# Adding the residual y on VectorE instead of by TensorE transposes, with two new work orders

## The chip, the cores and the metric

The kernel runs on one core of a Trainium2 chip, in float32. The metric is device microseconds of one launch; the median over runs is compared. Engines are named as the profile names them: PE is TensorE (PEld its weight loads), DVE is VectorE, ACT is ScalarE, POOL is GpSimd, and SP issues most of the DMAs.

## The reference, cut to what matters

Two layers follow each other on x of shape (4, 64, 64, 256): four batches of 4096 tokens with 256 channels. The first is a self-attention over the 4096 tokens of a batch with a residual. The second is triangle attention with 8 heads, a residual, a layer norm, an MLP and a second layer norm.

```python
# layer 0, per batch
s = einsum('bqd,bkd->bqk', g, f); beta = softmax(s); o = (beta @ v) @ Wo + bo
y = x + o
# layer 1, per batch
scores = einsum('bilhd,bljhd->biljh', q, k) / sqrt(32); att = softmax(scores, axis=2)
out = einsum('biljh,bilhd,bljhd->bijhd', att, v1, v2)
h = y + out.reshape(B, N, N, E) @ Wo1
h = layer_norm(h) * ln_agg_g + ln_agg_b
z = relu(h @ W1 + b1) @ W2 + b2 + h
result = layer_norm(z) * ln_out_g + ln_out_b
```

The change concerns the line `h = y + ...`: y is held with channels on the partitions, and the heads' product has tokens there, so y has to be turned before it is added.

## The kernel before, in words

The program is one list of instructions for each engine, written in a fixed order (`tc.manual_schedule()`); every engine works through its own list in order and waits on semaphores. For each batch b there is an attention stage (`layer0`) and a triangle stage (`first_layer1` for b = 0, `next_layer1` for b = 1 to 3). A closing stage (`Tokens.alone`) ends the program.

**Attention stage.** 8 blocks of 512 queries (`qb`), each of 8 groups (`k`, counted through as `g`). A group makes scores `s` on PE (L552), exponentials `e` on ACT (L564, buffers of tag `k8`, two of them), products `o` on PE (L579), and a running sum `esum` on DVE (L586). The work that follows a block is spread over the groups of the next block by the list `parts`: normalisation at k = 0 (`norm`, with the sums split in two by L594 to L596 into the one buffer of tag `hid`), `output` at k = 1, where DVE makes y (L632) and SP stores it to DRAM with channels as rows (L635), and projections q, k, v1 and v2 for the triangle stage at k = 2 to 7. In batch 0 DVE also turns the later batches' x by 32x32 blocks (L356). In batches 2 and 3, `recall`, `settle`, `rooted`, `polished`, `scaled` and `finish` bring back the MLP results of the batch two before and do their last layer norm; before the change one 256-token tile goes through them every 3 groups. `finish` is the last scale and shift, two operations on POOL (L1287, L1288) and a store to the output.

**Triangle stage.** 32 steps: 4 pairs of heads times 8 groups of 8 rows. A step has 8 products R = att x v2 of 128x2048 (`product`, L1007, words `R`); for batches 1 to 3 DVE makes 5 and POOL 3 in an even step, and 6 and 2 in an odd one. PE sums each with a 32-column stationary tile (`accumulate`, L1017, words `A`). R has 3 buffers for DVE and 2 for POOL. DVE also makes the softmax sums (`sums`, L932 and L934, words `S`), ACT the weights (`W`), PE turns them (`t`).

**Tokens.** Beside the steps of batch b, the 16 tiles (256 tokens each) of batch b-1 go through the second half of layer 1. `load` fetches a tile's attention output A and, before the change, `yc`, its y with channels on the partitions. `heads` (words h0, h1) makes `hp` in PSUM: two products with Wo1 for each half (L1120), and then two matmuls with the identity (L1125) that turn y and add it in the same accumulation. `sa` makes mean and variance: in batches 1 and 2 by sums on ACT (`sums_of`), in the last stage by bn_stats on DVE. Then `rr`, `pp` (small steps on ACT and POOL), `fa` (normalise), `ht`, `hT` (turn and scale), `m`, `r` (first MLP product, ReLU), `z` (second). In batches 1 and 2 the results are stored (`carried_off`, `summed_off`) and finished in a later attention stage; in the last stage they are finished at once, with `finish` on POOL.

**Order.** In the triangle stages the lists ORDER and ORDER_LAST say in which order the words of one period (two steps and one tile) are written; `/1` or `/2` means that the word works on the period one or two before, `/-1` on the one after. 20 periods are written. First and second tile of a batch have their heads in the last part of `layer0`.

**Closing stage.** `alone` takes the last batch's tiles 2 to 15 through heads, MLP and both norms, one per iteration, with the tiles' `A` and y fetched far ahead.

Of the kernel before, what the change touches and what calls it, by code (L numbers as in the profile page):

```python
# [18 lines left out]
P = 128  # L19
# [24 lines left out]
    R03/2 R06/2 t1/2 h0 m0/1 R04/2 c1/2 A03/2 A07/2 R16/2 A04/2 A06/2 R12/2 R10/2 T00/2 fi/2 W0/1 sf/2 R17/2  # L44
    T01/2 A10/2 A12/2 t0/1 R11/2 r0/1 fo/2 R13/2 R15/2 f1/2 h1 m1/1 f0/2 A11/2 c0/1 A16/2 V0/1 R14/2 r1/1 A13/2
    A15/2 R00/1 A17/2 T10/2 A14/2 sp/1 R02/1 sa R05/1 e0/1 R01/1 z0/1 rr/1 T11/2 z1/1 pp/1 e1/1 so/1 A00/1 A05/1
    R07/1 W1/1 A02/1 A01/1 fa S1 ht V1/1 S0 hU hT
# [4 lines left out]
    r0/1 A10/2 A11/2 m1/1 R14/2 R05/1 S1/1 R15/2 T10/2 sp/1 A14/2 A16/2 r1/1 e0/1 e1/1 A15/2 A05/1 T11/2 R04/1  # L52
    A04/1 z0/1 W1/1 R03/1 V1/1 fi/2 S0 z1/1 t1/1 so/1 R06/1 R00/1 c1/1 sa A03/1 R07/1 R02/1 A06/1 A02/1 A00/1
    rr/1 pp/1 W0 R01/1 A07/1 A01/1 fo/1 fa T01/1 R12/1 t0 T00/1 R17/1 h1/-1 sf/1 R13/1 h0/-1 f0/1 ht f1/1 R16/1
    hU A13/1 hT A12/1 A17/1 R11/1 c0 R10/1 m0 V0
# [19 lines left out]
def attention_then_triangle_kernel(  # L75
# [44 lines left out]
    nc.gpsimd.memset(back_t, -1.0)  # L120
    nc.gpsimd.memset(back_t[:, 2:4], -16.0)
# [85 lines left out]
    dens = ctile([P, NB, 256 + 16], "dens")  # L207
# [238 lines left out]
    class Late:  # L446
# [5 lines left out]
        def load(self, q):  # L452
            self.y = []
            for cc, tag in enumerate(("A", "yc")):
                t = work.tile([P, 512], F32, tag=tag, name="yb", bufs=1)
                nc.sync.dma_start(out=t, in_=self.io["y"][ts(cc, P), ts(q, 512)])
                self.y.append(t)
            self.used = 0
# [39 lines left out]
    def layer0(b, F, safe, rest, ahead):  # L498
# [8 lines left out]
        io["v1"] = dram.tile([T, C], F32, tag="v1", name="v1d")  # L507
        L = Layer1(b, io, safe)
# [105 lines left out]
        def bounds(qb):  # L614
            for j, (t, op) in enumerate(ends.pop(qb)):
                if not safe:
                    c0 = 256 + 2 * qb + j
                    nc.vector.tensor_reduce(dens[:, b, c0 : c0 + 1], t, AX.X, op)
# [7 lines left out]
        def output(qb):  # L626
            col = ts(qb, QB)
            o = oT.pop(qb)
            for cc in range(2):
# [5 lines left out]
                nc.sync.dma_start(out=io["y"][ts(cc, P), col], in_=y(qb, cc))  # L635

# [91 lines left out]
        if late:  # L728
# [4 lines left out]
            parts[7] = [lambda qb: proj(qb, "k", 1)]  # L733
        last = NQB - 1
        for r in range(4):
            score(0, r)
        for g in range(8 * NQB):
# [22 lines left out]
            if b > 1:  # L760
                for do, late in ((rest.finish, 7), (rest.scaled, 6), (rest.polished, 5), (rest.rooted, 4), (rest.settle, 3), (rest.recall, 0)):
                    if (g - late) % 3 == 0 and 0 <= g - late < 3 * NP:
                        do(NP * (b - 2) + (g - late) // 3)
# [29 lines left out]
        bounds(last)  # L793
        proj(last, "v2", 0, None, stage[1][:, 0, :], nc.scalar)
# [55 lines left out]
    class Layer1:  # L850
        def __init__(self, b, io, safe):
# [5 lines left out]
            self.R, self.begun, self.acc, self.rec, self.e = {}, {}, {}, {}, {}  # L857

# [62 lines left out]
        def sums(self, step):  # L921
# [8 lines left out]
            else:  # L930
                den = dens[:, self.b, ts(step, IG)]
# [112 lines left out]
    class Tokens:  # L1044
        def __init__(self):
            self.ios = []
            self.A, self.htp = {}, {}
# [47 lines left out]
        def load(self, tt, far=False):  # L1095
# [4 lines left out]
            if far:  # L1100
# [3 lines left out]
                A, yc = both[:, 0].rearrange("p c (i j) -> p c i j", j=N), both[:, 1]  # L1104
            else:
                A = work.tile([P, 2, 4, N], F32, tag="A", name="A", bufs=1)
                yc = work.tile([P, 2, 256], F32, tag="yc", name="yc", bufs=1)
# [3 lines left out]
            nc.sync.dma_start(out=yc, in_=io["y"][:, ts(t, 256)].rearrange("(c p) t -> p c t", p=P))  # L1111
            self.A[tt] = A, yc

        def heads(self, tt, n, psum=pb, new=None):
# [3 lines left out]
            A, yc = self.A[tt]  # L1118
            for cc in range(2):
                nc.tensor.matmul(  # L1120
                    hp[:, n, :], A[:, cc, ts(n, 2), :].rearrange("p i j -> p (i j)"), wo1_sb[:, cc, :],
                    start=(cc == 0), stop=False,
                )
            for cc in range(2):
                nc.tensor.matmul(  # L1125
                    hp[:, n, ts(cc, P)], yc[:, cc, ts(n, P)], ident, start=False, stop=(cc == 1),
                    is_transpose=True,
                )
# [10 lines left out]
        def stats_a(self, tt):  # L1139
# [539 lines left out]
```

## Time and profile before

| | |
|---|---|
| time, median of 3 runs | 3630.94 us (3627.85 to 3633.84) |
| profiled execution | 3633.17 us, of which the span is 3631.4 us |
| PE busy | 3522.3 us, 97% |
| DVE busy | 2823.5 us, 78% |
| ACT, POOL busy | 1923.8 us, 1779.2 us |
| PE clock granted | 0.994 |

The stages stand at about 0 to 470 us (attention, batch 0), 470 to 860 (triangle 0), 860 to 1300 (attention 1), 1300 to 1730 (triangle 1), 1730 to 2155, 2155 to 2580, 2580 to 3018 (attention 3), 3018 to 3480 (triangle 3, the last) and 3480 to the end (closing stage).

In a timeline line the first number is the start and the second the length in microseconds, and `xN` counts merged instructions. In a line of a group, "busy" counts each moment once, and "mean ns of one" is the length of one instruction, which can overlap its neighbours'. Matmuls in float32 are two PE instructions each; transposes are one.

### The profile page before, as it was taken

How to read it: one execution, taken by the hardware profiler on the slowest of the kernel's cores; microseconds unless marked ns; L12 is line 12 of the kernel's file. 1: busy time of each engine (PE TensorE's matmuls, PEld its weight loads, DVE VectorE, ACT ScalarE, POOL GpSimd, SP SyncE). 2: the span in 40 equal slices, each digit the busy share in tenths (PEclk: the TensorE clock that was granted, in tenths of full speed). 3: DMA queues.
4: the chain of work that ended last, by engine and by line, in shares of the span. 5: the costliest groups of instructions: out<-in, count | busy, mean ns of one | idle time of the engine just before them, and what ended most of it. 6: DMA issues, size and time to landing. Idle time of an engine off the chain costs nothing.

```text
span 3631.4 us, 58644 instructions
## 1 busy us (share of the span) xinstructions
PE 3522.3 (97%) x22282; PEld 1895.3 (52%) x22282; DVE 2823.5 (78%) x2558; ACT 1923.8 (53%) x4221; POOL 1779.2 (49%) x904
## 2 busy tenths in 40 slices
PE   9999999988999999999999999999899999999998
PEld 6555444434555555554455555554455555555477
DVE  4777499996555569999777549999877756999976
ACT  3444455544444366665444446666444436777655
POOL 5000099995000068889211018889611106999920
PEclk9999999999999999999999999999999999999999
DMA  9544555455111354425423254343622235441221
GB/s 174 135 131 127 136 151 137 122 134 136 47 52 52 82 145 108 101 68 107 110 91 95 67 146 109 89 104 76 132 87 95 80 93 134 92 96 46 68 68 55
DMA packets 492594, 370.15 MB, mean 102 GB/s; under 512 B 303184, under 2 KB 434000, under 8 KB 483472
## 3 DMA queue, kind: packets, MB, share of 16 engines
q1 hardware_dynamic: 443264, 339.36, 34.8%
q0 software_dynamic: 36160, 19.94, 5.3%
q10 hardware_dynamic: 12880, 7.01, 0.7%
q8 instruction: 178, 2.92, 0.4%
q14 instruction: 112, 0.92, 0.1%
HBM read 205.73 MB, written 160.43 MB: 101 GB/s over the span
## 4 chain that ended last, share of the span: by engine, by line
PE 67%; POOL 8%; DVE 6%; issue 4%; ACT 1%; DMA 1%; SPq 0%; ACTq 0%; POOLq 0%; DVEq 0%
PE o L579 16%; PE acc L1017 16%; POOL Rp L1007 7%; PE proj L646 6%; PE mp L1253 5%; PE zp L1273 5%; PE s L552 4%; PE sp L905 3%; PE hp L1120 3%; DVE R L1007 2%; PE v1p L678 2%; PE att L959 1%; PE y L631 1%; DVE rec L608 1%; PE htp L1220 1%
## 5 line engine op out<-in xcount | busy, mean ns | idle before, releaser
L1007 POOL TENSOR_TENSOR Rp<-attP,v 128x2048 f32<-128x2048 f32 x328 | 1491.4, 4579 | 409.7 <-ACT attP L967 367.0
L1007 DVE TENSOR_TENSOR R<-att,v 128x2048 f32<-128x2048 f32 x696 | 1546.1, 2279 | 68.6 <-PE acc L1017 49.9
L579 PE MATMUL o<-e,v 128*128 128x512 f32 x2048 | 1043.9, 593 | 0.0
L586 DVE TENSOR_TENSOR esum<-esum,e 128x2048 f32<-128x2048 f32 x224 | 518.8, 2316 | 398.4 <-ACT e L564 395.9
L564 ACT ACTIVATE e<-s 128x1024 f32<-128x1024 f32 x512 | 522.3, 1023 | 529.2 <-PE s L552 438.7
L552 PE MATMUL s<-gT,fT 128*128 128x512 f32 x1024 | 786.7, 770 | 8.7 <-ACT e L564 4.7
L1017 PE MATMUL acc<-R,wsel 128*32 128x512 f32 x5568 | 702.8, 599 | 26.5 <-DVE R L1007 19.6
L579 PEld LDWEIGHTS o<-e,v 128*128 128x128 f32 x2048 | 388.2, 190 | 276.8 <-issue 234.0
L1027 ACT COPY ao<-acc 128x1024 f32<-128x1024 f32 x256 | 256.4, 1013 | 290.4 <-PE acc L1017 205.8
L1017 PE MATMUL acc<-Rp,wsel 128*32 128x512 f32 x2624 | 344.3, 596 | 25.6 <-POOL Rp L1007 23.2
L1017 PEld LDWEIGHTS acc<-R,wsel 128*32 128x32 f32 x5568 | 155.5, 109 | 393.7 <-issue 273.9
L552 PEld LDWEIGHTS s<-gT,fT 128*128 128x128 f32 x1024 | 194.5, 190 | 244.7 <-issue 230.8
L1287 POOL TENSOR_TENSOR hz<-hz,log_bc 128x512 f32<-128x512 f32 x32 | 47.1, 1471 | 542.8 <-ACT hz L1197 474.4
L1181 POOL TENSOR_SCALAR nt<-mv 128x2 f32<-128x2 f32 (+1 forms) x49 | 9.4, 192 | 565.2 <-DVE mv L1137 560.1
L942 ACT ACTIVATE es<-S,rd 128x64 f32<-128x64 f32 x1024 | 258.3, 338 | 15.0 <-DVE rd L934 13.1
L1253 PE MATMUL mp<-hT,w 128*128 128x256 f32 x1024 | 244.4, 384 | 1.7 <-ACT hT L1225 1.7
L1273 PE MATMUL zp<-w,hid 128*128 128x256 f32 x1024 | 239.4, 384 | 0.8 <-ACT hid L1262 0.8
L1253 PEld LDWEIGHTS mp<-hT,w 128*128 128x128 f32 x1024 | 186.5, 190 | 53.0 <-ACT attP L967 12.6
L1273 PEld LDWEIGHTS zp<-w,hid 128*128 128x128 f32 x1024 | 188.0, 190 | 47.8 <-issue 14.7
L608 DVE RECIPROCAL rec<-den 128x512 f32<-128x512 f32 x32 | 107.4, 3357 | 109.7 <-PE den L604 104.4
L1017 PEld LDWEIGHTS acc<-Rp,wsel 128*32 128x32 f32 x2624 | 80.7, 110 | 214.1 <-issue 144.9
L915 ACT ACTIVATE S<-sp 128x512 f32<-128x512 f32 x128 | 131.6, 1094 | 78.0 <-PE sp L905 78.0
(192 smaller groups left out, 3688.4 us busy)
## 6 DMA issues: line engine op xcount, KB each, us to landing
v<-v2d SPq DMA_DIRECT2D x44, 512.0 KB
v1c<-v1d SPq DMA_DIRECT2D x128, 128.0 KB
aT<-ao SPq DMA_DIRECT2D x1024, 16.0 KB
A<-aT SPq DMA_DIRECT2D x256, 64.0 KB
hz<-raw SPq DMA_DIRECT2D x32, 512.0 KB
y<-yT SPq DMA_DIRECT2D x56, 256.0 KB
q<-st SPq DMA_DIRECT2D x56, 256.0 KB
k<-st SPq DMA_DIRECT2D x52, 256.0 KB
```

The source lines that it names most:

```text
L552: nc.tensor.matmul(s_ps[r // 2][:, r % 2, :], fT[tt][:, ts(r * 4 + n, P)], gT[qb // 4][:, ts(qb % 4, QB)], start=True, stop=not safe,)
L564: nc.scalar.activation(e[g][:, 2 * j : 2 * j + 2, :], s_ps[j], AF.Exp)
L579: nc.tensor.matmul(o_ps[qb], F.v[tt][:, r * 4 + n, :], es[:, r, :], start=(k == 0 and r == 0), stop=(k == 7 and r == 3),)
L586: nc.vector.tensor_tensor(esum[qb], esum[qb], es, ALU.add)
L608: nc.vector.reciprocal(rec, den)
L646: nc.tensor.matmul(ps, w[:, cc, rows], y(qb, cc), start=(cc == 0), stop=(cc == 1))
L942: nc.scalar.mul(e[:, i, :], rows[:, i, :], rec[:, i : i + 1])
L1007: eng.tensor_tensor(R, src.unsqueeze(1).to_broadcast([P, D, N]), v2[h], ALU.mult)
L1017: nc.tensor.matmul(acc[32 * c : 32 * c + 32, n % 2, :], w[:, n, c, 16 * h : 16 * h + 32], R[:, ts(c, 8), :].rearrange("p d j -> p (d j)"), ...
L1027: nc.scalar.copy(self.ao[step][:, ts(np, 2)].rearrange("p k d j -> p k (d j)"), self.acc[step][np])
L1253: nc.tensor.matmul(self.mp[:, fc % 2, :], w1_sb[:, cc, ts(fc, P)], self.hT[tt][:, cc, :], start=(cc == 0), stop=(cc == 1),)
L1273: nc.tensor.matmul(zp[:, n, :], self.hid[tt][:, fc, ts(n, P)], w2_sb[:, fc, :], start=(fc == 0), stop=(fc == 3 and tt not in self.hT2),)
```

## The change

- In `layer0`, `turn_y` lets DVE turn each block of y: 8 transposes of 128x128 elements by 32x32 blocks, at k = 5 of the next block, into a tile of tag `hid`. SP then stores it by 4 DMAs to a new DRAM tensor `yt`, with tokens as rows, in pieces of 64 channels (256 bytes). The last block's tile takes a `k8` buffer, and its 4 DMAs are issued by `L.owed()` at the second period of the triangle stage.
- `load` fetches `yt` (tokens on the partitions, two buffers) in place of `yc`. `heads` has no identity matmuls. `add_y` adds y to `hp` in PSUM on DVE, two operations of 128x256 ahead of the mean and variance of each tile, in all triangle stages and the closing stage.
- In the last triangle stage `sa` sums on ACT, as in batches 1 and 2. The last scale and shift of its 16 tiles is no longer done there: the tiles are stored, and `alone` brings back two per iteration and finishes them on POOL.
- In the attention stages of batches 2 and 3, two tiles go through the recalled work in each block at set groups (recall at k = 0 and 1, settle at 3 and 4, finish of both at 7).
- ORDER and ORDER_LAST are new lists; a special case for the first period of the last stage is gone. The softmax sums of a batch are reduced to limits once per batch, instead of all at the end.

```diff
 ORDER = """
-    R03/2 R06/2 t1/2 h0 m0/1 R04/2 c1/2 A03/2 A07/2 R16/2 A04/2 A06/2 R12/2 R10/2 T00/2 fi/2 W0/1 sf/2 R17/2
-    T01/2 A10/2 A12/2 t0/1 R11/2 r0/1 fo/2 R13/2 R15/2 f1/2 h1 m1/1 f0/2 A11/2 c0/1 A16/2 V0/1 R14/2 r1/1 A13/2
-    A15/2 R00/1 A17/2 T10/2 A14/2 sp/1 R02/1 sa R05/1 e0/1 R01/1 z0/1 rr/1 T11/2 z1/1 pp/1 e1/1 so/1 A00/1 A05/1
-    R07/1 W1/1 A02/1 A01/1 fa S1 ht V1/1 S0 hU hT
+    sa R11/2 A13/2 A10/2 A11/2 T01/2 R12/2 sp/1 r0/1 e0/1 e1/1 t0/1 m1/1 R14/2 A12/2 A17/2 fo A14/2 R00/1 V0/1
+    R16/2 T10/2 r1/1 A16/2 c0/1 S1/1 W1/1 rr/1 R07/1 R15/2 A00/1 A15/2 z1/1 R01/1 T11/2 z0/1 pp/1 t1/1 R03/1
+    A01/1 R02/1 so/1 fa A07/1 A03/1 c1/1 R06/1 A02/1 ht hT S0 hU T00/1 fi/1 R05/1 h1/-1 V1/1 h0/-1 m0 R04/1
+    R13/1 W0 sf/1 R10/1 A04/1 A06/1 A05/1 f0/1 R17/1 f1/1
 ORDER_LAST = """
-    r0/1 A10/2 A11/2 m1/1 R14/2 R05/1 S1/1 R15/2 T10/2 sp/1 A14/2 A16/2 r1/1 e0/1 e1/1 A15/2 A05/1 T11/2 R04/1
-    A04/1 z0/1 W1/1 R03/1 V1/1 fi/2 S0 z1/1 t1/1 so/1 R06/1 R00/1 c1/1 sa A03/1 R07/1 R02/1 A06/1 A02/1 A00/1
-    rr/1 pp/1 W0 R01/1 A07/1 A01/1 fo/1 fa T01/1 R12/1 t0 T00/1 R17/1 h1/-1 sf/1 R13/1 h0/-1 f0/1 ht f1/1 R16/1
-    hU A13/1 hT A12/1 A17/1 R11/1 c0 R10/1 m0 V0
+    f0/2 A17/2 A12/2 R14/2 R15/2 r0/1 T10/2 W1/1 m1/1 r1/1 R05/1 sp/1 R04/1 A14/2 A16/2 e0/1 e1/1 A15/2 sa R06/1
+    S0 A05/1 V1/1 T11/2 W0 A04/1 R03/1 z1/1 z0/1 R02/1 so/1 rr/1 t1/1 c1/1 A03/1 R00/1 A06/1 A02/1 R01/1 A00/1
+    R11/1 R07/1 S1 pp/1 fa A07/1 R13/1 A01/1 ht fo/1 R17/1 hU hT t0 R10/1 h0/-1 fi/1 c0 T01/1 T00/1 h1/-1 V0 m0
+    sf/1 A13/1 R12/1 A11/1 R16/1 A10/1 f1/1
...
+        def turn_y(qb, **where):
+            t = work.tile([P, 16, 2, 32], F32, name="yr", **where)
+            for cc in range(2):
+                rows = y(qb, cc).rearrange("p (k t) -> p k t", t=32)
+                for k in range(4):
+                    nc.vector.transpose(t[:, ts(k, 4), cc, :], rows[:, ts(k, 4), :])
+            def kept():
+                for r in range(4):
+                    nc.sync.dma_start(
+                        out=io["yt"][ts(qb, QB), ts(r, 64)].rearrange("(k t) c -> t k c", t=32),
+                        in_=t[ts(r, 32)].rearrange("t k h c -> t k (h c)"),
+                    )
+            return kept
...
+        parts[5].append(lambda qb: turn_y(qb, tag="hid", bufs=1)())
...
+                for t in range(2):
+                    for do, at in (
+                        (rest.recall, t), (rest.settle, 3 + t), (rest.rooted, 4 + t), (rest.polished, 5 + t),
+                        (rest.scaled, 6 + t), (rest.finish, 7),
+                    ):
+                        if k == at:
+                            do(NP * (b - 2) + 2 * qb + t)
...
+        L.owed = turn_y(last, tag="k8")
...
-            nc.sync.dma_start(out=yc, in_=io["y"][:, ts(t, 256)].rearrange("(c p) t -> p c t", p=P))
+            nc.sync.dma_start(out=yt, in_=io["yt"][ts(t, 256)].rearrange("(n p) c -> p n c", p=P))
...
-            for cc in range(2):
-                nc.tensor.matmul(
-                    hp[:, n, ts(cc, P)], yc[:, cc, ts(n, P)], ident, start=False, stop=(cc == 1),
-                    is_transpose=True,
-                )
+        def add_y(self, tt):
+            hp, yt = self.hps[tt], self.yt.pop(tt)
+            for n in range(2):
+                own = hp[:, n, :].rearrange("p (h r c) -> p h r c", h=2, r=4)
+                nc.vector.tensor_tensor(own, own, yt[:, n, :].rearrange("p (r h c) -> p h r c", h=2, r=4), ALU.add)
...
         def stats_a(self, tt):
+            self.add_y(tt)
             self.stats(self.hps[tt], 0)
...
+        def fetched(self, tt):
+            b, t = divmod(tt, NP)
+            self.z[tt] = work.tile([P, 2, C], F32, tag="R", name="zr", bufs=3)
+            nc.sync.dma_start(out=self.z[tt], in_=self.raw[b][t][:, 1])
...
         def alone(self, t0, t1):
+            late = list(range(NP * (NB - 2), NP * (NB - 1)))
+            brought = []
...
+                for one in brought:
+                    self.finish(one)
+                brought, late = late[0:2], late[2:]
+                for one in brought:
+                    self.fetched(one)
...
-                if own:
-                    rest.stats(rest.hps[tt], 0)
-                else:
-                    junk = work.tile([P, 2, C], F32, tag="sx", name="junk", bufs=1)
-                    rest.sums_of(rest.hps[tt], junk, rest.mv, 0)
+                rest.add_y(tt)
+                junk = work.tile([P, 2, C], F32, tag="sx", name="junk", bufs=1)
+                rest.sums_of(rest.hps[tt], junk, rest.mv, 0)
...
-                (rest.finish if own else rest.summed_off)(tt)
+                rest.summed_off(tt)
...
-                if own and i == 0 and word in ("A05", "A04"):
-                    for m in (4, 5) if word == "A04" else ():
-                        step_word("A", 0, m)
-                elif word[0] in "RATSWVtc":
+                if word[0] in "RATSWVtc":
                     step_word(word[0], 2 * i + int(word[1]), int(word[-1]))
```

## The prediction

> **What bounds the kernel now.** First the page's head and its busy line, to see which engine could hold the span:
>
> ```profile
> span 3631.4 us, 58644 instructions
> PE 3522.3 (97%) x22282; PEld 1895.3 (52%) x22282; DVE 2823.5 (78%) x2558; ACT 1923.8 (53%) x4221; POOL 1779.2 (49%) x904
> ```
>
> PE is the bound nearly everywhere, so PE time that goes is worth its full length, unless another engine is close behind. Averages hide that, so next the windows: one steady period of triangle stage 1 and one of the last stage (columns: stretch, length, then busy PE, PEld, DVE, ACT, POOL):
>
> ```profile
> 1359.10:1386.21 27.11, 27.11 (x250) 14.52 (x249) 26.04 (x16) 17.93 (x51) 24.11 (x12) 1.00 0.22 59
> 3169.06:3196.82 27.76, 27.76 (x256) 14.96 (x260) 26.87 (x20) 19.69 (x54) 26.64 (x15) 1.00 0.20 50
> ```
>
> PE is busy without a gap, but DVE is only about 1 us behind it, and the change takes from PE and gives to DVE. Third, the timeline of PE and DVE in such a period, for the spacing of instructions (start, length):
>
> ```profile
> 1394.29 1.03 PE L1120 MATMUL hp<-wo,A 128*128 128x256 f32 x4
> 1395.15 0.38 PE L1125 MATMUL hp<-ident,yc 128*128 128x128 f32 x2
> 1395.37 1.91 PE L1253 MATMUL mp<-hT,w 128*128 128x256 f32 x8
> ```
> ```profile
> 1389.53 0.69 DVE L932 TENSOR_REDUCE dens<-S 128x8 f32<-128x512 f32 x1 [0.57 <-ACT S L915]
> ...
> 1391.15 6.64 DVE L1007 TENSOR_TENSOR R<-att,v 128x2048 f32<-128x2048 f32 x3
> 1398.35 17.71 DVE L1007 TENSOR_TENSOR R<-att,v 128x2048 f32<-128x2048 f32 x8 [0.56 <-PE acc L1017]
> ```
>
> Two identity matmuls hold PE for 1395.37 - 1395.15 = 0.22 us, though each is 0.27 long. DVE idles 0.57 + 0.56 = 1.13 of 27.11, so its work is 26.0. Fourth, the chain that ended last: the last periods of stage 1 hang on POOL, at a pitch of 27.2 (1687.43 - 1660.25):
>
> ```profile
> 1660.25 9.06 POOL Rp L1007 x2
> 1679.68 4.56 POOL Rp L1007
> 1687.43 9.04 POOL Rp L1007 x2
> ```
>
> Last the groups by form, for the prices (busy total, mean ns):
>
> ```profile
> L1125 PE MATMUL hp<-ident,yc 128*128 128x128 f32 x200 | 38.2, 273 | 0.0
> L1125 PE MATMUL hp<-ident,A 128*128 128x128 f32 x56 | 10.7, 273 | 0.0
> L356 DVE STREAM_TRANSPOSE xr<-xr 128x128 f32<-128x128 f32 x192 | 48.6, 388 | 0.0
> L1343 DVE TENSOR_TENSOR z<-zp,z 128x256 f32<-128x256 f32 x2 | 0.8, 404 | 0.0
> ```
>
> **The change, part by part.**
>
> *Identity matmuls off PE.* 4 per tile, 64 tiles: 4 x 0.109 = 0.43 us a tile, 27.9 us in all. This, not the 48.9 us that the two groups show as busy, is the ceiling. The Trainium skill ("TensorE: Matmul & The Clock Gate", Part 4: PE-mode transpose) gives about 275 ns for such a transpose inside a kernel; by that 256 of them would be an estimated 70 us. The lengths here agree (273), the spacing is less than half, and spacing decides.
>
> *The add on DVE.* Two operations of 128x256, PSUM and SBUF in. The nearest row is L1343, 0.40 to 0.42. In the built instruction list the second add waits for the first, so they do not overlap: a dependent neighbour of that size starts 0.46 after (3622.98 and 3623.44 in the closing stage). Pair: 0.46 + 0.40 = 0.86 us. Below: two independent ones, 0.7 (512-element operations start 0.61 apart where they are independent, 267 ns of it elements). Above: 0.75 each, what 128x512 with three inputs takes (L632), 1.5. I take 0.86.
>
> *Stages 1 and 2, steady.* PE: 27.11 - 0.43 = 26.68; the number of changes between its tile shapes stays 7 a period in the new list. DVE: 26.0 + 0.86 = 26.86, and becomes the bound. Does it still wait? I laid the new words of one period along DVE (an R every 2.21, sums 0.8) and along PE with the spacings above. With A11 at time X after the add, A15 needs R15 (X at least 3.3) and the reuse of the third R buffer needs A13 done before R12 of the next period (X at most about 4.3). A window of 1 us in which neither waits; at the signal times of 0.1 to 0.2 that the gaps show, some of it goes. I take 26.9: 0.21 gained in each of 12 periods, in two stages, 5.0 us. Ends: no wait at all 0.25 x 24 = 6; the add at 1.5, period 27.5, a loss of 9; the old 1.13 of idle stays, period 28.0, a loss of 0.9 x 24 = 21. The four periods behind them hang on POOL, whose work there is unchanged: 0.
>
> *Last stage, steady.* PE loses 0.43, and the new list has 7 instead of 9 changes of tile shape, 0.1 each: 1.92 for 8 MLP matmuls between two changes (3189.14 to 3191.06) against 1.84 with one. The old difference between the stages confirms this price: 27.76 - 27.11 = 4 more transposes (0.43) and 2 more changes (0.2). New period 27.13. DVE: 27.07 of work, minus bn_stats and aggregation (3175.32 to 3176.47, 1.15), plus 0.86: 26.8, just under PE. ACT takes the sums, two times 0.39 + 0.21 + 0.49 + 0.22 = 2.6 us: 19.7 + 2.6 = 22.3, not a bound. POOL loses `finish`, 1.29 + 1.29: 24.1. So 0.63 x 11 periods = 6.9. The three last periods, at 27.21 on POOL, gain 0.2 each as POOL is relieved: 0.6. At the start A05 now comes first, and waits for POOL's 4.55 us product where A04 ran before: -0.8. Sum 6.7.
>
> *Closing stage.* Pitch 9.51 (3515.21 to 3524.72), PE without gaps, DVE busy two thirds. 14 tiles x 0.43 = 6.0. The add lengthens the chain to the next tile's turn, which has over 5 us of room once running (h ready at 3499.4, turned at 3505.1); at the stage's first tile it is bare, -0.8. Finishing two tiles on POOL per iteration, 4 operations of 1.29 to 1.73 (5.2 to 6.9 us) and their loads, fits into 9.1; SP waits for POOL before it issues the next fetch and the output store queued behind that, whose buffer is wanted two iterations (18 us) later. If that cover went, 0.8 us per iteration would show for 8 iterations, 6 us. Sum 5.2.
>
> *Heads in the attention stages' ends.* 6 tiles. The three first ones lie in front of an output matmul that waits for DVE's 3.36 us reciprocal (PE waits 0.29 there already): 0. The other three: 1.3.
>
> *Turning y.* 8 transposes start to end 2.02 us (eight of L356 at 254.38), 64 us in all, in attention stages where DVE is busy 51 to 67%. At k = 5 of batch 0, the fullest group, DVE has 2.3 for `esum`, 2.0 for x and now 2.0, of about 6.1: it fits, and e's two buffers allow a slip of another group. Hidden, 0. Their stores stand on SP behind that group's projection stores and ahead of x's (batch 0); the four at the second period wait for nothing by then. 4 x 128 KB in 256-byte pieces: the nearest row is the store v2d<-sx of 256 KB in such pieces, 5.13 us on the chain, so about 10.3 for the block. Issue about 1052.0, and the next write of `hid` (`part`, at 1058.97) then waits until 1062.3, 3.3 us, with `esum` and the normalisation queued behind it on DVE. The denominators on PE came 5 us after `part` (DVE waited 5.10 for them): covered, with under 2 us to spare.
>
> *Recalled tiles and limits.* The two finishes at k = 7 of the last block end just before the buffer they free is written (about 9 us later, by sums along DVE's chain 2121.37 to 2132.29): 0, at worst 1 us twice. Limits move work of 1.27 us that nothing waited for: 0.
>
> The Trainium skill speaks against this change ("VectorE: DVE Perf Modes", Rules for kernel authors): a 128x128 transpose belongs on TensorE where a PSUM destination will do, and VectorE's own is for 32x32 blocks. In engine time the rows agree: 64 + 64 x 0.86 = 119 us of DVE replace 28 of PE. By the rule, with nothing of DVE's time hidden, the kernel would become 91 us slower; it gains only where DVE was idle.
>
> Sum: 5.0 + 6.7 + 5.2 + 1.3 = 18.2 us. From the profiled execution, 3633.2 - 18.2 = 3615.0; that one is 2.2 above the median, so 3612.7 against 3630.9.
>
> **The rivals.**
>
> *The most it can be (0.08).* Every steady period at its floor (6 + 6.9 + 6.0 + 1.3 = 20.2), the POOL periods pulled to DVE's 26.86 too (11 x 0.35 = 3.9) and some 5 of the few waits in the attention stages gone with the new spacing of recalled tiles: 29 us, 3602.
>
> *DVE keeps its idle (0.13).* Stages 1 and 2 run at 28.0 and lose 21, the rest gains 13.2: 3639 at that end; half of the idle kept, 3629. For it: DVE was already 96% busy and has 3 buffers. Against it: the window above.
>
> *The y stores hold `hid` (0.09), slower.* Place: `part` in each of 28 blocks, DVE blocked in front of `esum` and the normalisation. It decides from a landing of about 12 us after first issue (cover 5 us behind 1058.97). Price: each microsecond beyond is 28 us; at 13.5 us, 42 - 18 = 24 us slower, 3655. For it: 7 of the blocks are in batch 0, where DMAs are 60% busy already. Against it: 5.13 us for half the bytes.
>
> *That the transposes stay on PE* is out: the built list has no identity matmul of `heads` left.
>
> **How the numbers follow.** Forecast 3613, chance 0.70, its own range 3605 to 3622. A measurement here tells 0.2% (7.3 us) from no change. Faster: 0.70 + 0.08 = 0.78. Of the idle rival's 0.13, 0.08 lies within 0.2% and 0.05 above. Slower: 0.05 + 0.09 = 0.14. The range from 3602 to 3630 leaves out the stores' case and the upper half of the idle one.
>
> **What would show it.** Periods of stages 1 and 2 near 26.9 with DVE over 26.7 busy; of the last stage near 27.1 with PE full; a closing pitch near 9.1; the add pair at 0.86; DVE's wait at `part` for a DMA, at most 4 us, and PE without a wait at den. The forecast is wrong if a period of stage 1 is 27.1 or more, or PE waits for `e` or den in the attention stages.

## The result and the profile after

The changed kernel takes 3657.3 us (median of 4 runs, 3655.3 to 3660.4) against 3632.4 for the kernel before on the same chip. The ratio is 1.0072, with a 95% interval from 1.0057 to 1.0087: slower by 0.7%, where 3613 was forecast. The time is also outside the range of 3602 to 3630.

First the head and the busy line of the changed kernel's page. PE has lost 18 us of work and DVE has got 116; yet the span is 24 us longer, so PE stands idle about 42 us more than before.

```profile
span 3655.6 us, 58803 instructions
PE 3504.0 (96%) x22026; PEld 1870.9 (51%) x22026; DVE 2939.9 (80%) x2886; ACT 1954.7 (53%) x4349; POOL 1783.1 (49%) x903
```

Next the windows of a steady period of triangle stage 1 and of the last stage, for the two that the prediction showed. The lengths came out near the forecast: 26.80 (26.9 forecast, 27.11 before) and 27.28 (27.13 forecast, 27.76 before), with DVE's work 0.3 behind the period in the first.

```profile
1359.70:1386.50 26.80, 26.71 (x248) 14.13 (x244) 26.54 (x18) 18.07 (x51) 24.14 (x13) 1.00 0.23 60
3104.00:3131.28 27.28, 27.28 (x249) 14.53 (x248) 26.63 (x18) 21.29 (x63) 24.18 (x13) 1.00 0.19 49
```

So the loss is not in the steady work. Marks along PE show where it is. "Start" is from the last score matmul of an attention stage to the second MLP product `zp` of the third tile; "steady" the nine periods from there; "end" from there to the next attention stage, or in the last stage to the first `zp` of the closing stage. All times are from the two profiled executions, in us.

| part | before | after | difference | forecast |
|---|---|---|---|---|
| four attention stages | 1523.5 | 1518.6 | -4.9 | -1.3 |
| triangle 0 | 467.1 | 473.8 | +6.7 | 0 |
| stages 1, 2: starts | 102.2 + 102.2 | 107.1 + 112.0 | +14.7 | 0 |
| stages 1, 2: steady | 244.0 + 244.0 | 241.5 + 241.2 | -5.3 | -3.8 |
| stages 1, 2: ends | 128.5 + 128.5 | 130.5 + 130.3 | +3.8 | -1.2 |
| last stage: start, steady, end | 107.9 + 249.9 + 135.0 | 112.8 + 245.6 + 130.7 | -3.7 | -6.7 |
| closing stage to the last `zp` | 141.2 | 153.4 | +12.2 | -5.2 |

(The forecast of 5.0 for the steady periods covers 12 of them a stage; the table's nine have 3.8, the rest stands with the ends.) The rows make 23.5 of the 24.2 us. Three kinds of places hold the loss: triangle 0, the starts, and the closing stage, each a seam or a stage of its own.

**Closing stage.** The timeline of POOL and DVE shows an iteration that finishes recalled tiles (start, length). DVE's small operation on `nt` has length 1.13 in place of 0.16 us. It ends at 3542.55, within 0.02 us of POOL's product (3541.25 + 1.28); the next held one, 1.11 long, ends at 3543.90, as POOL's next does (3542.61 + 1.27).

```profile
3541.25 1.28 POOL L1320 TENSOR_TENSOR zr<-zr,log_bc 128x512 f32<-128x512 f32 x1
3542.61 1.27 POOL L1321 TENSOR_TENSOR zr<-zr,lob_bc 128x512 f32<-128x512 f32 x1
```
```profile
3541.23 0.16 DVE L1208 SCALAR_TENSOR_TENSOR nt<-mv,rs 128x2 f32<-128x2 f32 x1 [0.60 <-ACT rs L1198]
3541.42 1.13 DVE L1209 SCALAR_TENSOR_TENSOR nt<-nt,rs 128x2 f32<-128x2 f32 x1
3542.59 0.16 DVE L1210 SCALAR_TENSOR_TENSOR rn<-nt,rs 128x2 f32<-128x2 f32 x1
3542.79 1.11 DVE L1211 SCALAR_TENSOR_TENSOR rn<-mv,rn 128x2 f32<-128x2 f32 x1
```

The add itself, with one operand in PSUM, is not held (its row beside POOL stands with e5 below). The waits of PE in that stage show who passes the delay on: ACT's `hT` and `hid`, which come behind the statistics that DVE makes.

```profile
PE mp L1286 <- ACT hT L1258: 9.3, 6, 1.8
PE zp L1306 <- ACT hid L1295: 6.4, 5, 1.8
```

**Start of stage 1.** DVE's line shows the add as the first thing in the period, blocked for 7.67 us until PE has made the heads' product; the first R comes behind it, and PE waits 3.37 us for that R.

```profile
1308.07 0.90 DVE L1160 TENSOR_TENSOR hp<-hp,yt 128x256 f32<-128x256 f32 x2 [7.67 <-PE hp L1151]
1308.91 2.29 DVE L1038 TENSOR_TENSOR R<-att,v 128x2048 f32<-128x2048 f32 x1
```
```profile
1311.35 1.06 PE L1048 MATMUL acc<-R,wsel 128*32 128x512 f32 x8 [3.37 <-DVE R L1038]
1312.34 5.41 PE L1306 MATMUL zp<-w,hid 128*128 128x256 f32 x16
```

**Triangle 0.** PE's timeline has one wait that the kernel before has not:

```profile
450.79 2.60 PE L936 MATMUL sp<-q,k 32*64 32x64 f32 x64 [4.56 <-DMA k<-k]
```

### The profile page after: what moved, and what is told of

It is laid out like the page before. It is cut to its first block, busy times and chain, and to the rows that moved or that the text cites. A ratio compares the mean times of both kernels' runs of the same rounds, so it can differ in the third digit from the quotient of the medians.

```text
span 3655.6 us, 58803 instructions
## 1 busy us (share of the span) xinstructions
PE 3504.0 (96%) x22026; PEld 1870.9 (51%) x22026; DVE 2939.9 (80%) x2886; ACT 1954.7 (53%) x4349; POOL 1783.1 (49%) x903
## 4 chain that ended last, share of the span: by engine, by line
PE 63%; POOL 15%; DVE 10%; issue 6%; ACT 2%; DMA 2%; SPq 0%; ACTq 0%; POOLq 0%; DVEq 0%
PE o L585 23%; POOL Rp L1038 13%; PE acc L1048 10%; PE proj L668 8%; PE s L558 6%; DVE R L1038 5%; PE mp L1286 3%; PE sp L936 3%; PE v1p L700 2%; PE zp L1306 2%; PE y L637 2%; PE hp L1151 1%; PE att L990 1%; DVE st L1168 1%; PE v1p L438 1%
## 5 line engine op out<-in xcount | busy, mean ns | idle before, releaser
L1286 PE MATMUL mp<-hT,w 128*128 128x256 f32 x1024 | 244.4, 384 | 10.6 <-ACT hT L1258 10.6
```

Of the source, the lines that this page charges most:

```text
L1286: nc.tensor.matmul(self.mp[:, fc % 2, :], w1_sb[:, cc, ts(fc, P)], self.hT[tt][:, cc, :], start=(cc == 0), stop=(cc == 1),)
```

## The experiments

Every kernel below is an edit of the changed one. Times of one kernel lie up to 0.4% apart (e2: 3642.1 to 3655.7), so stage lengths of the profiles decide where an effect is a few microseconds. These move too: where the code of the stage is that of the changed kernel, the start of stage 1 is 105.4 to 108.4 (seven profiles), that of stage 2 is 108.5 to 112.0, and that of the last stage 110.3 to 112.8. The theory is that the losses are separate ones at the seams, and that the add costs nothing in the steady periods. The rival is that DVE's 116 us more work is the cause, and that what is mended in one place is waited for in the next.

### Closing stage (e3, e5, e6, e8)

```diff
-                rest.summed_off(tt)
+                (rest.finish if own else rest.summed_off)(tt)
...
-                for one in brought:
-                    self.finish(one)
-                brought, late = late[0:2], late[2:]
-                for one in brought:
-                    self.fetched(one)
```

> The last triangle stage finishes its own tiles on POOL again, as before the change, and the closing stage brings none back. Everything else is the changed kernel. Theory (POOL beside DVE): the closing stage's pitch of 10.0 to 13.1 us in its first 8 iterations comes from the recalled tiles alone, since DVE's operations with two SBUF operands run until POOL's end when they meet. Then the pitch is 9.2 us in all iterations, and the closing stage takes 140 us instead of 153.4 from the end of the last stage (141.2 before the change). The last stage takes POOL's 2.6 us more per period: 26.7 of 27.3, so at most its last five periods become longer, by up to 0.6 each. Time 3644 to 3648. Rival (chain): the add of y ahead of the statistics makes the chain to the next turn longer than an iteration; then the pitch stays at 10 or more in all iterations and little is gained.

Measured: 3641.0 us, ratio to the kernel before 1.0029 (1.0019 to 1.0039). The closing stage took 138.2 us, at a pitch (the time from one iteration to the next) of 9.1 to 9.2 behind the first one; the last stage's end became 134.3 instead of 130.7. The recalled tiles cost 15 us in the closing stage. What is left of its gain is 3.0 us (141.2 before), where the prediction had 5.2: the pitch fell from 9.5, and near the end PE waits 1.54 us for `hid`. The time fell somewhat further than forecast.

e5 and e6 keep e3 and add work for POOL that nobody uses:

```diff
+                if t0 < tt < t0 + 9:
+                    for _ in range(4):
+                        nc.gpsimd.tensor_tensor(idle, idle, log_bc.unsqueeze(1).to_broadcast([P, 2, C]), ALU.mult)
```

> Built on e3_no_late_finish, whose closing pitch was 9.2 us without any recalled tile. In the second to ninth iterations of the closing stage POOL gets four extra products of 128x512 (SBUF tile by the scale row, as the recalled finish had), on a private tile that nobody reads or loads; their result is not used. Theory (POOL beside DVE): neither the fetch nor the store of the recalled tiles was the cost, but two engines that read two SBUF operands each at the same time; the pitch of these eight iterations rises to 10 to 12 us, the closing stage from 138 to about 148, and DVE's 128x512 operations and the small ones of 0.16 us show lengths above 1 us. Rival (transfers): the fetches, stores and waits of SP made the long iterations; then the pitch stays 9.2 and the stage 138 us.

> As e5_pool_two_inputs, but the four extra operations are copies of the scale row into the private tile (one SBUF operand in place of two). If what counts is that POOL has two SBUF operands, the pitch stays at 9.2 to 9.5 us and the closing stage at 138 to 140. If any work of POOL on SBUF holds DVE, the pitch rises as in e5 by the time these copies take.

Measured: POOL ran the 32 products without a break in 45.8 us, and the closing stage took 155.3 us, 17 more than e3. The 32 copies took 23.7 us, and the stage 139.5. No transfer belongs to either, so POOL's work alone makes the loss; the rival of SP and transfers falls. DVE's timelines show the same operations, first beside products of 1.27 us (e5, with POOL's row and with an add that stands in the midst of it), then beside copies of 0.61 (e6); alone each of the first two takes 0.69:

```profile
3477.08 45.77 POOL L1359 TENSOR_TENSOR idle<-idle,log_bc 128x512 f32<-128x512 f32 x32
3496.70 0.90 DVE L1160 TENSOR_TENSOR hp<-hp,A 128x256 f32<-128x256 f32 x2
3502.07 1.77 DVE L1277 TENSOR_TENSOR z<-h,lag_bc 128x512 f32<-128x512 f32 x1
3503.87 1.64 DVE L1278 TENSOR_TENSOR z<-z,lb_bc 128x512 f32<-128x512 f32 x1
```
```profile
3504.34 1.11 DVE L1277 TENSOR_TENSOR z<-h,lag_bc 128x512 f32<-128x512 f32 x1
3505.48 0.98 DVE L1278 TENSOR_TENSOR z<-z,lb_bc 128x512 f32<-128x512 f32 x1
```

In the same run the add keeps its 0.90, and the sum of `zp` and z, which also reads PSUM, its 0.68. Copies hold DVE too, and less. They were done by 3509 us, in the first iterations, where e3 too has one of 11.5, so e6 does not say what as many microseconds of copies would cost later. The expectation that the second operand decides is wrong: the extra lengths are about 1.0 and 0.35.

In e8 (with the edits of e2 and e4 below) the recalled tiles stay in the closing stage, on DVE:

```diff
+                for one in brought:
+                    self.finish(one, V)
+                n = 2 if tt < t0 + 2 else 1
```

> As e7_three_mended, but the closing stage keeps the recalled tiles, with their last scale and shift on DVE in place of POOL, one tile per iteration (two in the first two), and the last triangle stage is the changed one. DVE then has 6.1 + 1.4 of 9.2 us per iteration. Theory: with POOL silent no operation is stretched, the pitch is 9.2 to 9.4 us and the closing stage takes 138 to 141 us; the last stage's end is 3.6 us shorter than with the own finish (e3), so the time is 0 to 3 us below e7. Rival (DVE's chain): any 1.4 us more on DVE ahead of the statistics delays the next turn, as the stretched operations did; the pitch is 10 or more and the time 8 or more above e7.

Measured: 3645.7 us, ratio 1.0038 (1.0024 to 1.0051), a pitch of 10.5 in the iterations with one tile; the closing stage took 157.5. The rival was right: 1.38 us more on DVE gave 1.35 us more pitch. In the windows of one such iteration neither engine is full (PE 9.37, DVE 8.75 of 10.50):

```profile
3562.00:3572.50 10.50, 9.37 (x46) 7.82 (x45) 8.75 (x26) 5.26 (x14) 0.00 (x0) 1.00 0.44 126
```

So the pitch is a loop. In such an iteration DVE waits only twice, 0.60 us each, for ACT's roots, and the same holds in e3, where DVE is busy 7.48 of 9.13 us (3538.37 to 3547.50) and PE all of it. DVE's chain with its waits is thus as long as PE's work, and has no slack, since its idle time is inside the chain. What e8 put on it showed in full.

### End of the attention stages (e2)

The edit puts back the old distance (one tile every 3 groups):

```diff
-                for t in range(2):
-                    for do, at in (
-                        (rest.recall, t), (rest.settle, 3 + t), (rest.rooted, 4 + t), (rest.polished, 5 + t),
-                        (rest.scaled, 6 + t), (rest.finish, 7),
...
+                    if (g - wait) % 3 == 0 and 0 <= g - wait < 3 * NP:
+                        do(NP * (b - 2) + (g - wait) // 3)
```

> The recalled tiles in the attention stages of batches 2 and 3 go back to one tile every 3 groups, so that the last is finished 10 groups before the stage's end. Theory (freed buffer): in the changed kernel the last two outputs are stored at the stage's very end, and VectorE waits up to 3.1 us for those stores before it may write the buffer `stage` (5.1 us in two waits); triangle stages 2 and 3 start that much later. Then the stretch from the last score matmul of the attention stage to the first second-MLP product falls from 54.7 to about 50.5 us in stage 2 and from 55.9 to about 53 us in stage 3, 6 to 7 us together, and 1 to 3 us of it are given back in the two attention stages (386.5 to 388). Time about 3652. Rival: these starts are late because the y add stands first on VectorE; then they stay at 54 to 56 us.

Measured: the start of stage 2 went from 112.0 to 107.2, of the last stage from 112.8 to 106.4; 1.6 and 1.7 us came back in the two attention stages. The time, 3654.4 us with ratio 1.0065 (1.0049 to 1.0082), does not tell these 8 us from none, so the verdict rests on the stage lengths. As these move without the edit too, the safer pair is e4 and e7, where the granted clock stays at 1.00 behind the first R: 105.9 against 102.6 in stage 2, 110.3 against 106.4 in the last stage, 7.2 us together. The reason was only half right. Beside the wait for the freed buffer (2.0 us in stage 2) it is POOL again: in the changed kernel the two finishes ran beside DVE's last sums, which PE's denominators wait for (first fence, sums from 2131.93 on); in e2 they had been done (second fence).

```profile
2131.93 2.17 DVE L595 TENSOR_TENSOR esum<-esum 128x1024 f32<-128x1024 f32 x1
2134.14 1.63 DVE L597 TENSOR_TENSOR esum<-esum 128x512 f32<-128x512 f32 x1
```
```profile
2126.38 1.23 DVE L595 TENSOR_TENSOR esum<-esum 128x1024 f32<-128x1024 f32 x1
2127.64 0.69 DVE L597 TENSOR_TENSOR esum<-esum 128x512 f32<-128x512 f32 x1
```

### Start of stages 1 and 2 (e4, e14)

```diff
+                if period == 1 and not own:
+                    if word in ("sa", "rr"):
+                        continue
+                    if word == "pp":
+                        of_piece("sa", 1)
+                        of_piece("rr", 0)
```

> In the second period of triangle stages 1 and 2 alone, the add of y, the sums and roots of the first tile come later, just ahead of its polish, behind two or three of the products R. Theory (blocked start): the new order has this add first, and VectorE stands 7.67 us for the heads' products of that tile (1308.1) before its first R, and PE then 3.37 us for that R. Then the first accumulation starts about 3.5 us sooner; stretch from the last score to the third tile's second-MLP product falls from 107.1 to about 103.5 us in stage 1 and from 112.0 to about 108.5 in stage 2, and the time by about 7, to 3650. Rival (POOL): the start is led by POOL's products and not by VectorE's, or what is gained there is lost again in the last periods, which hang on POOL; then the time falls by under 2 us.

Measured: 3646.2 us, ratio 1.0039 (1.0024 to 1.0053). The starts fell from 107.1 to 102.6 and from 112.0 to 105.9, 10.6 us together and more than the two waits of 3.3 to 3.4 us. In the changed kernel the granted clock fell behind both waits, in e4 in neither stage. Against profiles with the wait in which it did not fall (e2 and e9 with 105.4 in stage 1; e3, e5 and e9 with 108.5 to 108.7 in stage 2), e4's starts are 2.8 and 2.6 to 2.8 shorter. So some 5.5 us are the wait's, and some 5 the clock's and what else differs between two profiles. e14 leaves the wait and fills it:

```diff
                 accs[n // 2] = pa("acc")
+                if step == 0 and self.b in (1, 2) and not begun:
+                    for _ in range(3):
+                        nc.tensor.matmul(
+                            accs[n // 2][:, 0, :], ident, w1_sb[:, 0, :], start=True, stop=True
+                        )
```

> The changed kernel with 3 matmuls of 128x512 on constants ahead of the first accumulation of triangle stages 1 and 2, where PE stood 3.4 us for the first R; their result is overwritten. The wait itself stays (R comes at the same time), but PE is busy in it. Theory (clock): the wait is what halved the granted clock behind it; filled, the clock stays at 1.0 in these places, the 16 matmuls of the first zp behind it take 3.8 us instead of 5.41, and from the last score to the third tile's second product stage 1 takes 105.4 us instead of 107.1, stage 2 one to three less than 112.0. Rival: the clock falls there for the load and not for the wait; then 5.4 us and 107 stay.

The windows of two microseconds behind that wait, first of the changed kernel, then of e14. The column after POOL's is the granted PE clock: 0.71 and 0.50 against 1.00. The third fence is e14's PE, the fourth that of e9, where the wait is not filled.

```profile
1312.00:1314.00 2.00, 2.00 (x9) 1.41 (x6) 2.00 (x2) 1.94 (x9) 0.00 (x0) 0.71 1.02 284
1314.00:1316.00 2.00, 2.00 (x6) 1.55 (x6) 2.00 (x2) 0.48 (x3) 1.00 (x5) 0.50 0.97 205
```
```profile
1312.00:1314.00 2.00, 2.00 (x12) 1.62 (x9) 2.00 (x2) 2.00 (x9) 0.00 (x0) 1.00 1.05 288
1314.00:1316.00 2.00, 2.00 (x12) 1.72 (x12) 2.00 (x2) 0.37 (x3) 1.15 (x6) 1.00 0.94 217
```
```profile
1311.20 1.06 PE L1053 MATMUL acc<-R,wsel 128*32 128x512 f32 x8 [0.80 <-DVE R L1038]
1312.20 3.72 PE L1311 MATMUL zp<-w,hid 128*128 128x256 f32 x16
```
```profile
1306.56 1.06 PE L1048 MATMUL acc<-R,wsel 128*32 128x512 f32 x8 [3.38 <-DVE R L1038]
1307.56 3.72 PE L1306 MATMUL zp<-w,hid 128*128 128x256 f32 x16
```

R came when it came before (PE took it at 1311.20 against 1311.35), but the matmuls behind it took 3.72 instead of 5.41 us, and the start of stage 1 105.4 instead of 107.1, of stage 2 109.1 instead of 112.0. This does not show that the filling did it. The unfilled wait of 3.3 to 3.4 us stands 14 times in seven profiles (stages 1 and 2 of the changed kernel, e1, e2, e3, e5, e6 and e9). Nine times the clock fell to 0.50, and the 16 matmuls took 4.35 to 5.82 us. Five times it stayed at 1.00 (stage 1 of e2 and e9, stage 2 of e3, e5 and e9), and they took 3.72, as in e14; the start of stage 1 is 105.4 in e2 and e9 too. Two filled waits without a fall can be chance, so e14 leaves open whether useless work keeps the clock up. What the profiles show is the price of a fall: starts of stage 1 of 106.9 to 108.4 instead of 105.4, that is 1.5 to 3 us. (The one run took 3650.9 us.)

### Triangle 0 (e1, e9)

e1 keeps the seventh block's stores until the eighth's are issued; e9 leaves the block out:

```diff
+            kept = turn_y(qb, tag="hid", bufs=1)
+            if b == 0 and qb == last - 1:
+                owed.append(kept)
+            else:
+                kept()
```
```diff
-        parts[5].append(lambda qb: turn_y(qb, tag="hid", bufs=1)())
+        parts[5].append(lambda qb: turn_y(qb, tag="hid", bufs=1)() if b or qb != last - 1 else None)
```

> Only in batch 0 the four stores of the seventh block's turned y are held until the second period of the triangle stage, when the eighth block's go out too. Theory (queue): these 4 x 128 KB stand on SP ahead of the loads of q, k and v2 for the triangle stage, whose queue is full there; the k load for the second pair of heads landed at 450.5 us instead of before 447, and PE waited 4.6 us for it. Then that wait goes, triangle stage 0 takes 469 us instead of 473.8 (467.1 in the kernel before), and the time falls by 4 to 5 us against the changed kernel, to about 3653. Rival (work): stage 0 became longer since VectorE has 2 us more to do per block; then it stays at 473 to 474 and the time does not move.

> The changed kernel without the seventh block of batch 0 in the turning: its 8 transposes and 4 stores are left out, and two tiles of that batch (12 and 13) get the rows of the block before instead, so 512 tokens have another y. All else is the same. e1, which held these stores until the triangle stage's second period, took away the wait of PE for the k load (4.6 us), but a wait of 6.4 us came up elsewhere: the held buffer is the one that the next batch's g and f go through. Theory (queue): the loads at the stage's end are late because 0.5 MB in 256-byte pieces stands ahead of them in a full queue; without it the k load is in time, PE does not stand in front of the score products at 446, and the stretch from 404 to 470 us is 4 to 5 us shorter than in the changed kernel (its first products of the step after at 463 to 464 instead of 468.3). Triangle stage 0: 466 to 469 us. Rival (DVE): the first R come late for another reason; then the wait stays.

Measured: the wait for the k load is in every other profile with these stores (13 of them, 4.6 to 6.2 us), and in neither e1 nor e9, nor before the change. So these stores make the load late. SP's own rows show how: it issues that pair's loads, q first, from 442.66 us on in the changed kernel, from 436.23 before, 435.50 in e1 and 436.94 in e9. The worth is not exact. In e1 PE waited 6.4 us a little later (1.7 in the changed kernel), for nothing that the profile names, and the stage took 471.3 us; e1 (3655.1 us, ratio 1.0064, 1.0047 to 1.0081) is inconclusive. In e9 the score products came without a wait at 447.69, and the stage took 467.5 (one run, 3649.9 us). But the stage moves from 468.1 to 476.3 between profiles in which it has the same stores, so 467.5 says little more than that the wait is gone: about 5 us.

### All together, and the order lists (e7, e10, e11, e12, e13)

e7 has the edits of e2, e3 and e4.

> The changed kernel with three edits together: own tiles finished in the last triangle stage as before the change (e3), recalled tiles in the attention stages at the old distance (e2), and the first add of triangle stages 1 and 2 behind the first products (e4). Theory (seams): the losses are in separate places, so the gains add: closing and last stage -12 (e3: 153.4 to 138.2, and 3.6 longer tails), starts of stages 2 and 3 -10 less 3 given back (e2), starts of stages 1 and 2 another -6 (e4, part of it shared with e2). From 3657 that is 3657 - 12 - 7 - 6 = 3632, with 3626 to 3636 as the clock falls: no slower than the kernel before, and about what the gains of the steady periods are worth below it. Rival (one limit behind all): what is mended in one place is waited for in the next, for instance by POOL at the stages' ends; then it stays above 3640.

Measured: 3628.75 us (11 runs), ratio to the kernel before 0.9990 (0.9981 to 0.9999). The three mends add up: 28 us below the changed kernel, and the starts are 102.5 and 102.6, those of before. The rival (DVE's work as such) falls: e7 has all of that work. It beats both kernels, the one before by a tenth of a per cent.

e10 does the add with everything else as before the change:

> The y add on DVE alone: y turned in the attention stages, fetched with tokens on the partitions and added by DVE as in the changed kernel, but both old ORDER lists, the old distance of recalled tiles, bn_stats in the last triangle stage and its tiles finished there, as before the change. By the prediction's prices the periods of stages 1 and 2 have 26.0 + 0.86 = 26.86 us of DVE's work, and in the last stage 27.07 + 0.86 = 27.93 against 27.76 before. Theory (the lists made room): the old order leaves DVE's two waits of 1.13 us in the period, so stages 1 and 2 run at 27.4 to 28.0, the last at 28.0 to 28.6, the closing stage at 9.2 (138 to 139 us), the stages' starts and ends as before; 3640 to 3655 in all. Rival (the lists were not needed): DVE's waits shrink by what the add takes, the periods are 26.9 and 27.9, and the time is 3628 to 3634.

Measured: 3708.9 us, ratio 1.0218 (1.0202 to 1.0233). Periods of 29.5 in stages 1 and 2, beyond the expected end of 28.0, and 27.8 in the last stage, no longer than before: there the rival's expectation held, in stages 1 and 2 neither. In DVE's waits in stage 1 (1330 to 1620 us), the wait for PE's `acc` was 9.5 us before the change in the same stretch:

```profile
DVE R L1037 <- PE acc L1047: 17.0, 18, 1.3
DVE dens L962 <- ACT S L945: 5.5, 2, 2.8
DVE R L1037 <- ACT attP L997: 5.3, 8, 0.7
```

With the add on DVE, the new ORDER is thus worth 2.7 us a period, 65 us over two stages. The tight list turned a bound of 26.86 into a period of 26.8; without it the add would have cost far more than it saved.

What is left of the new list's price was tried at both ends. e11 writes what remains after 14 periods in the old list's order:

```diff
+            words = [w for w in words if w[2] < 14]
+            done = {w[0:2] for w in words}
+            words += [w for w in listed(ORDER_ENDS) if w[0:2] not in done]
```

> e7_three_mended (3628.75 us) with the ends of triangle stages 1 and 2 in the old order: periods 0 to 13 are written by the new list, and what is then left by the old one. Theory (ends): the last four periods of these stages have the same work but another order; the old one took 104.5 us for four second-MLP products and 24.0 to the next stage, the new one 108.6 and 21.8, so the end becomes 1.9 us shorter in each stage, and the time 3 to 4 us less, about 3625. Rival (POOL): POOL's products, at 4.55 us each, bound the end whatever the order, and what counts is how far POOL has come before; then nothing moves, or the seam between the lists costs a microsecond or two more.

Measured: 3636.9 us, ratio 1.0014 (1.0005 to 1.0023). The ends became longer, 110.8 + 24.2 against e7's 108.6 + 21.8. e12 and e13 begin with two and four periods of the old list in the same manner:

> As e7_three_mended (3628.75 us), but triangle stages 1 and 2 begin with two periods in the old order, and what is left then follows in the new list's order; the first add is where the old list has it. Theory (first periods): the new list's first periods cost 3.7 us a stage, since its words stand in the order of a full period when half of them have nothing to work on yet; then the first five POOL products take 27 to 28 us instead of 30.7, the rest stays at 26.8 a period, and the time is 6 to 7 us below e7, about 3622. Rival (the seam): what is saved at the start is paid where the two lists meet, as at the ends (e11); then 3626 to 3632.

> As e12, with four periods in the old order. The old order with the add on DVE ran at 29.5 us a period (e10) against 26.8, so each further old period costs 2.7 us: by the theory of e12 the two stages are 5 us longer each than in e12. If the seam costs and not the number of old periods, they are as long as in e12.

Measured: e12 3635.9 us, ratio 1.0010 (1.0001 to 1.0019), starts of 108.4 and 105.9 against e7's 102.5 and 102.6 (with the 108.4 the granted clock fell too, in a wait of 1.91 us); e13 one run of 3641.1, starts of 106.0 and 106.2 and steady parts 3.6 to 4.7 longer. All three seams cost more than the part that they replaced. For e11 and e12 the rivals were right, though e12's time is beyond theirs; e13's longer steady parts fit the price of an old period from e10. Why the ends of stages 1 and 2 are 2 us longer than before stays open; in stage 1 PE's waits for POOL's Rp are 9.7 us there against 6.7.

## Why the prediction was wrong

**Right:** 0.43 us a tile off PE and 0.86 for the add (0.89 to 0.90). The steady periods, 26.80 and 27.28; but DVE, named as the bound with 26.86 of work, was busy 26.54, less than PE's 26.71. The transposes of y hidden in the attention stages, none of which became longer. The stores do not hold `hid` so that PE waits: the slower rival had another place than the real loss, though the same sign.

**Finishing two tiles on POOL per iteration "fits into 9.1"** is the step that failed most: 5.2 us were forecast as a gain of the closing stage, 12.2 were lost, and 15 of these 17 are the finishes (e3). POOL's time fits; what was not asked is what POOL's reading does to DVE. The page before had the sign: `hz` by `lb_bc` on DVE took 811 ns on average, where its neighbours of the same shape take 685 and 692: 4 of the 32 took 1.64 us, each beside a finish on POOL, the other 28 took 0.69. POOL's own finishes there took 1.27 to 3.20. The Trainium skill states the rule ("SBUF — State Buffer", Who interferes with whom): a DVE instruction with two SBUF inputs contends with a GpSimd instruction that reads SBUF, and the contention is an exclusive lock; a DVE instruction with at most one SBUF input, outside the 2-port modes, does not contend. The rows agree in both halves: 0.69 to 1.64 and 1.77 for two SBUF operands, 0.90 unmoved for the add in PSUM.

**"Over 5 us of room"** in the closing chain: there was none. The time between a ready h and its turn was read as free; e8 shows that 1.38 us more on DVE come out as 1.35. With no recalled tiles (e3) the stage gains 3.0 instead of 5.2.

**"0, at worst 1 us twice"** for the finishes at k = 7: 4.7 and 6.4 us at the two starts between the changed kernel and e2, 3.3 and 3.9 between e4 and e7, less 1.6 and 1.7 given back in the attention stages (e2). The buffer was priced, POOL beside DVE's last sums was not. The prediction had named the sign, a wait of PE at den: it became 3.1 us at the ends of attention stages 2 and 3, from 1.2.

**The starts** had no term at all but 0.8 in the last stage. The new list was judged by a full period. In the first one half of its words have nothing to do, and the one that remains in front, the add, blocked DVE for 7.67 us (e4).

**The stores of y in batch 0** were weighed against the buffer they hold, not against the loads queued behind them on SP, the k of the second pair of heads among them: about 5 us.

**The clock** was missing from every term. Behind the waits of PE for the first R it was halved in nine of 14 cases, for 3.4 or 6.8 us; of the 10.6 us that e4 gained in the profiles, some 5 are not the waits' own, and most of that is the clock by the 1.5 to 3 us that a fall costs in stage 1. What decides whether it falls stays open.

**Ends of stages 1 and 2:** forecast at 0 for POOL's unchanged work, 1.9 us longer each; open.

## What to carry to other kernels

A reordered list must be costed at its first and last periods, too, by walking each engine's list there: the word in front blocks all behind it. Work moved to an engine called idle must be priced for what it shares with its neighbour; a mean length above that of the same shape elsewhere is the sign to look for. Idle time inside a dependent loop is not slack. A gain read from one profile must be held against profiles of unchanged code: here the start of stage 1 moves by 3 us among seven of them, and an edit that seemed to save 1.7 us can't be told from that.

## What the runs showed of the hardware

- DVE operations with two SBUF operands and POOL's take turns: one of 0.69 us takes 1.64 to 1.77 beside POOL products of 1.27 (e5), and 0.98 to 1.11 beside copies of 0.61 (e6). Even one of 128x2 can take 1.1 instead of 0.16. POOL is held as well: 2.40 for a product of 1.27 beside DVE's sums. With one operand in PSUM DVE is not held: the pair of adds keeps its 0.90, and the products R, which read `att` from PSUM, take 2.28 us beside POOL's 4.58 us products (571 in the changed kernel, none over 2.30).
- Behind a PE wait of 3.3 to 3.4 us the granted clock fell to 0.50 in nine of 14 cases, for 3.4 us in five of them and 6.8 in four; in the other five it stayed at 1.00. The Trainium skill ("TensorE: Matmul & The Clock Gate", Part 1) has half rate after an idle window of about 3.4 us and full rate after as long a busy one, and calls the window free-running. The lengths of the falls agree, and so does that the same wait is followed by one in some executions only. That a full idle window must come first does not show: the falls began 2.0 to 4.9 us after PE had begun to wait, and in e12 one began within a wait of 1.91 us, with one of 0.82 and eight transposes before it.
